# Routing the last sequence's softmax transposes through HBM in a one-core attention + mixture-of-experts kernel

## The chip, the cores and the metric

The kernel runs on 1 core of one Trainium2 chip. The metric is the device time of one execution in microseconds (us), as the median of several runs. Before the change it is 686.94 us, the median of 3 runs (684.95 to 687.5).

## The reference

All numbers are float32. Eight sequences of 512 tokens with 256 features go through causal attention, and then every token goes through one shared feed-forward expert and two of eight routed experts:

```python
x = x + attn(layernorm(x), Wq, Wk, Wv)        # x: (8, 512, 256); one head, scores / sqrt(256), causal softmax
h = layernorm(x)
shared = (silu(h @ shared_gate.T) * (h @ shared_up.T)) @ shared_down.T       # inner size 512
probs = sigmoid(h @ router_w.T + routing_bias)                                # 8 experts
scores, indices = top_k(probs, 2); scores = scores / sum(scores)              # weights w per token and expert
routed = sum over the two experts e of w_e * ((silu(h @ gate_w[e]) * (h @ up_w[e])) @ down_w[e])
out = x + shared + routed
```

## The kernel before

A sequence is four blocks of 128 tokens (`NT` = 4), and the 256 features are two chunks of 128 (`ND` = 2). Wq and Wk are folded into one matrix ahead of everything, so that a sequence needs one projection for its scores (`project_q`) and one for its values (`project_v`).

**First stage, one iteration per sequence b (0 to 7).** For each of its four blocks i, `attend` multiplies the transposed exponentials with the values ("average", tile `av`, with i + 1 pairs of matmuls), adds the result to the residual (`summed`, line 476), works out the second layer norm (statistics on VectorE, a power on GpSimd) and normalizes into `hn`. Scores and exponentials of sequence b + 1 are made at the end of iteration b. There are two ways to turn things around, because the array needs its contracted index on the partitions:

- on TensorE: `attend` transposes the exponentials block by block (line 463), and `turned` transposes `hn` (line 340); each result is copied out of PSUM by ScalarE;
- by HBM: the tile is written to HBM and read back in 32-row strips (`stored_rows`, `loaded_blocks`, `loaded_squares`), and VectorE then transposes 32 x 32 squares (`turn_squares`, `turn_exponentials`, line 434).

Three sets say which sequence goes which way. `SENT` are the sequences whose exponentials go by HBM: 1 to 6 before. `VIA` and `WHOLE` are those whose `hn` goes by HBM, its first half or all of it: `WHOLE` is 0 to 5; sequence 6 turns all of `hn` on TensorE, sequence 7 its second half.

**Routing.** The generator `chosen` runs `route` in pieces: logits on TensorE (`lT`, 16 records), their transpose (`pl`), the first of the two choices on VectorE, then the second choice and the running counts (`run`, line 535). `place` works out each token's row in a table in HBM (`pp`, `at`), and `dispatch` scatters the rows with eight indirect transfers from GpSimd (line 559, `rows_h`). Before, sequence 6 does its whole routing at once at the end of its iteration.

**The shared expert beside it.** `shared_beside` does the shared expert for half a sequence (a "unit"): for each of four chunks m a gate and an up product (`pg`, line 578; w = 0 and 1), a tanh on ScalarE (line 589) and two VectorE instructions ("gates", lines 593 and 596, the second writes `hid`), and then two down products (`po`, line 605), each copied by ScalarE (line 609, `marks["sh"]`). In the trace each 128-row float32 matmul is two records, so a unit is 32 records of `pg` and 16 of `po`. Sequences 0 to 3 and 7 have their units in the list `waiting`; sequences 4 to 6 store `hT` and get their shared expert after the routed experts. Before, one unit is done in each iteration 0 to 5 and one in iteration 7; the three that are left come after the loop, beside `plan_tiles`.

**After the loop.** `plan_tiles` counts tokens per expert, writes blank rows (line 199) and makes a table of tiles. Then come the routed experts, tile by tile: `fetch` loads a tile's rows from `rows_h` with four strip loads and a `tail` on SyncE's queue (lines 851, 856), and its two expert matrices of 512 KB with two loads on ScalarE's queue (line 838). The first tile's rows wait until all scattered rows have landed. `turn` transposes (line 873), `expert_up` multiplies (line 900), ScalarE takes the silu (line 885), VectorE the product (line 886), `expert_down` multiplies again (line 923). Rows and weights are fetched three tiles ahead; the weights of tiles 1 and on are issued behind the last unit's `marks["sh"]` on ScalarE:

```python
        with tc.issue_after(opening), tc.issue_after(marks["sh"]):
            items += [fetch(t)[1] for t in range(1, AHEAD)]
        with tc.issue_after(marks["hid"]):
            hT = turn(0, items[0][0])
```

**What sets the order.** The order on each engine is fixed when the program is built, by the order of the code and by a planner that takes ready work where an engine would be idle. `with tc.issue_after(ins)` puts the block's instructions behind `ins` on the engine of `ins`; instructions on other engines are not held. `marks` carries such points between functions. PSUM is shared by three pools: `ps_t` (2 buffers, transposes), `ps_m` (4, most products), `ps_o` (2; `av`, `lT`, `pl`, `pp`, `po`).

Of the kernel before, what the change touches and what calls it, by code (L numbers as in the profile page):

```python
# [26 lines left out]
def kernel(  # L27
# [45 lines left out]
    assert B == E, "each sequence's attention has one expert's down weights loaded beside it"  # L73
    EARLY = B // 2
    LATE = range(EARLY, B - 1)
    VIA = [b for b in range(B) if b != B - 2]
    WHOLE = range(B - 2)
    SENT = range(1, B - 1)

    BLOCKS = NT * (NT - 1) // 2, NT  # L80
    RS = 1.0 / D ** 0.5
# [194 lines left out]
    with ExitStack() as first, ExitStack() as inner:  # L276
# [181 lines left out]
        def attend(xb, i, ex, inv, v, mv, rstd, hn, meanwhile=None, exT=None):  # L458
            n = (i + 1) * P
            if exT is None:  # L460
                pt = ps_t.tile([P, S], F32, tag="t", name="pt")
                for j in range(i + 1):
                    nc.tensor.transpose(pt[:, ts(j, P)], ex[:, ts(j, P)], ident)
                exT = work.tile([P, S], F32, tag="exT", name="exT")
                marks["exT"] = nc.scalar.copy(exT[:, :n], pt[:, :n]).ins
            else:
                exT = part(exT, i)
            if meanwhile is not None:
                meanwhile()
            av = ps_o.tile([P, D], F32, tag="o", name="av")  # L470
            for j in range(i + 1):
                mixed = nc.tensor.matmul(  # L472
                    av, lhsT=exT[:, ts(j, P)], rhs=v[:, j, :], start=(j == 0), stop=(j == i)
                )
            with tc.issue_after(marks["turned"]) if "turned" in marks else nullcontext():
                summed = nc.vector.scalar_tensor_tensor(
                    out=xb[:, i, :], in0=av, scalar=inv, in1=xb[:, i, :], op0=ALU.mult, op1=ALU.add
                )
            stats_of(mv, xb[:, i, :], i)
            power = rstd_of(rstd[:, i : i + 1], mv[:, i : i + 1, :])  # L480
            if i:
                with tc.issue_after(summed.ins) if i != NT // 2 or xb is not total[B - 1] else nullcontext():
                    normalize(hn[:, i - 1, :D], xb, i - 1, mv, rstd)
            return mixed.ins, summed.ins, power

        def route(b, hT, hn):


            lT = ps_o.tile([P, P], F32, tag="o", name="lT")
            for k in range(ND):  # L490
                for c in range(NT):
                    marks["routed"] = nc.tensor.matmul(
                        lT[ts(c, P // NT), :], lhsT=r_sb[:, k, :], rhs=hT[:, k, ts(c, P)],
                        start=(k == 0), stop=(k == ND - 1),
                    ).ins
            logits = small.tile([P, P], F32, tag="logits", name="logits", bufs=2)
            nc.scalar.copy(logits, lT)
            yield
            pl = ps_o.tile([P, NT, P // NT], F32, tag="o", name="pl")
            marks["routed"] = nc.tensor.transpose(pl.rearrange("p c e -> p (c e)"), logits, ident).ins  # L500
            pl = pl[:, :, :E]
            wide = [P, NT, E]
            prob = small.tile(wide, F32, tag="prob", name="prob")
            nc.vector.tensor_tensor(out=prob, in0=pl, in1=bias_sb.unsqueeze(1).to_broadcast(wide), op=ALU.add)
            nc.scalar.activation(prob, prob, AF.Exp, scale=-1.0)
            nc.vector.tensor_scalar_add(prob, prob, 1.0)
            nc.vector.reciprocal(prob, prob)
            here = ts(b, NT)
            for r in range(TOP):
                top, hot = tops[r][:, here], hots[r][:, here, :]  # L510
                if r:
                    yield
                with tc.issue_after(marks["turned"]) if r and b < B - 2 else nullcontext():
                    nc.vector.tensor_reduce(out=top, in_=prob, axis=AX.X, op=ALU.max)
                nc.vector.tensor_tensor(
                    out=hot, in0=prob, in1=top.unsqueeze(2).to_broadcast(wide), op=ALU.is_equal
                )
                nc.vector.tensor_tensor(out=hot, in0=hot, in1=order, op=ALU.mult)
                win = small.tile([P, NT], F32, tag="win", name="win")
                nc.vector.tensor_reduce(out=win, in_=hot, axis=AX.X, op=ALU.max)  # L520
                nc.vector.tensor_tensor(
                    out=hot, in0=order, in1=win.unsqueeze(2).to_broadcast(wide), op=ALU.is_equal
                )
# [14 lines left out]
            yield mask  # L538
# [22 lines left out]
                    in_=hn[:, c, :], in_offset=None,  # L561
                ))

        def shared_beside(b, half, hT, midway=None, behind=None, rows_from=NI, early=None, steps=(), halfway=None):


            n = S // 2
# [5 lines left out]
            for m in range(NI):  # L573
                pg = ps_m.tile([P, 2, n], F32, tag="m", name="pg")
                for w in range(2):
# [6 lines left out]
                    if (m, w) in steps:  # L582
                        with tc.issue_after(mm.ins):
                            next(early, None)
                            held = marks["routed"]
                    elif (m, w) == (NI // 2 - 1, 1) and halfway is not None:
                        held = halfway
                sg = beside.tile([P, n], F32, tag="sg", name="sg")
                nc.scalar.activation(sg, pg[:, 0, :], AF.Tanh, scale=0.5)  # L589
                with nullcontext() if early is None or not 0 < rows_from < NI and m < rows_from else tc.issue_after(  # L590
                    marks["half"] if m >= rows_from else marks["coming"]
                ):
                    nc.vector.scalar_tensor_tensor(
                        out=sg, in0=sg, scalar=1.0, in1=pg[:, 0, :], op0=ALU.add, op1=ALU.mult
                    )
# [34 lines left out]
        for b in range(B):  # L630
# [27 lines left out]
            for i in range(NT):  # L658
# [2 lines left out]
                rest = None  # L661
                if b in SENT:
                    sc = exs[i]
                    if i % 2 == 0:
                        with tc.issue_after(mixed) if i else nullcontext():
                            qT = project_q(ahead_T, range(i // 2 * ND // 2, (i // 2 + 1) * ND // 2), qT if i else None)
                elif i + 1 < NT:
# [23 lines left out]
                if i == 1 and added is not None and b not in SENT:  # L691
                    with tc.issue_after(summed):
                        added()
                    added = None
                if i == (1 if b in SENT else 2) and placed is not None:
                    placed()


# [55 lines left out]
            def chosen(b=b, hT=hT, hn=hn):  # L754
# [5 lines left out]
                next(routing)  # L760
                yield
                next(routing)
                if b < B - 2:
                    yield
                mask = next(routing)

# [6 lines left out]
            if b + 1 < B:  # L773
                choice = chosen()
                next(choice)
                if b + 2 == B:
                    for _ in choice:
                        pass
            else:
                added = shared_beside(*waiting.pop(0), early=chosen(), rows_from=0, halfway=mixed, steps=((NI // 2, 1), (NI - 1, 0), (NI - 1, 1)))  # L780
            if b in LATE:
                with tc.issue_after(marks["sent"]):
                    nc.sync.dma_start(out=hT_d[b], in_=hT)
# [1 line left out]
                waiting += [(b, 0, hT), (b, 1, hT)]  # L785
            if b + 1 < B:

                if b + 2 < B:
                    def behind():

                        nonlocal exT
                        with tc.issue_after(marks["hid"]), tc.issue_after(marks["first"]):
                            exT = turn_exponentials(squares)
                        next(choice, None)
                        marks["squares"], marks["turned"] = marks["turned"], marks["run"]

                    def midway():
                        if b + 3 < B:
                            with tc.issue_after(marks["squares"]):
                                rows, _ = first_norm(*coming)  # L800
                            with tc.issue_after(marks["sent"]):
                                blocks[b + 3], _ = sent_to_blocks(xn_d[b + 3], rows)

                    added = shared_beside(
                        *waiting.pop(0), midway=midway, behind=behind, early=choice,
                        rows_from=1 if b in WHOLE else NI,
                        steps=((NI // 2, 1), (NI - 1, 1)) if b in WHOLE else ((0, 1), (1, 1)),
                    )
                xT = ahead_T
        placed()  # L810
        for c in to_send:
# [316 lines left out]
```

## Time and profile before

| what | value |
|---|---|
| median of 3 runs | 686.94 us |
| profiled execution, time | 678.78 us |
| profiled execution, span from first to last instruction | 677.0 us |
| granted TensorE clock over the span | 1.00 |
| busy share: TensorE, VectorE, ScalarE, GpSimd | 98%, 45%, 22%, 23% |
| first stage, iterations 0 to 6 | up to about 198 us |
| iteration 7, plan, last units | about 198 to 259 us |
| routed experts, late shared experts, sums | about 259 to 677 us |

A profile line gives times from the start of the span. In the chain of waits each line is start, duration, engine and line of the step that the end was waiting for. In the timeline each line is start, duration, engine and line, operation, output <- inputs, count and, in square brackets, how long the engine had been idle and what ended that. An engine with a "q" is its instruction queue issuing a transfer.

### The profile page before, as it was taken

What the parts mean: (1) busy time and instruction counts of PE and PEld (TensorE: products, weight loads), DVE (VectorE), ACT (ScalarE), POOL (GpSimd) and SP (SyncE); (2) the same over time, 40 slices, a digit from 0 to 9 for tenths busy, and PEclk for the clock granted to TensorE, in tenths of its full rate; (3) what the DMA queues carried; (4) which work ended last, traced back from release to release, by engine and by line L of the source; (5) the groups of instructions that cost most, each with busy time, mean ns of one, the idle gap of its engine ahead of it and who ended that gap; (6) DMA issues with size and microseconds to landing.
All of it is one profiled execution on the core that took longest, in us unless ns stands there. A gap on an engine that the chain in (4) does not pass through costs nothing.

```text
span 677.0 us, 10380 instructions
## 1 busy us (share of the span) xinstructions
PE 663.7 (98%) x3170; PEld 542.0 (80%) x3170; DVE 301.9 (45%) x1004; ACT 149.6 (22%) x357; POOL 157.2 (23%) x210
## 2 busy tenths in 40 slices
PE   7999999999999999999999999999999999999998
PEld 5677787777776888888888888888888899984556
DVE  4678879779786853212212212122122112223665
ACT  3433231332223222121111111211111111111110
POOL 3103351533526520022112121111211122120000
PEclk9999999999999999999999999999999999999999
DMA  7665777867834367776555354463543457714775
GB/s 237 192 166 147 219 210 178 220 180 209 218 115 134 106 163 226 230 199 209 162 167 170 119 180 150 138 180 127 161 161 102 159 172 239 259 65 146 244 226 177
DMA packets 155529, 119.52 MB, mean 177 GB/s; under 512 B 111856, under 2 KB 134000, under 8 KB 155472
## 3 DMA queue, kind: packets, MB, share of 16 engines
q1 hardware_dynamic: 136272, 58.05, 32.8%
q10 hardware_dynamic: 12912, 43.53, 18.5%
q0 software_dynamic: 6288, 17.24, 7.0%
q8 instruction: 28, 0.46, 0.3%
q14 instruction: 29, 0.24, 0.1%
HBM read 83.31 MB, written 35.47 MB: 175 GB/s over the span
## 4 chain that ended last, share of the span: by engine, by line
PE 78%; DVE 9%; DMA 6%; SPq 2%; issue 2%; POOL 1%; ACT 1%; ACTq 0%; DVEq 0%; POOLq 0%
PE po L923 17%; PE pg L900 16%; PE pu L900 16%; PE pg L578 7%; PE po L605 4%; PE pg L1011 3%; PE po L1070 3%; PE pu L1011 3%; PE av L472 3%; PE sc L442 2%; PE pm L407 2%; PE pm L395 2%; SPq L377 2%; DVE bnst L172 2%; DMA blocks<-hnd 2%
## 5 line engine op out<-in xcount | busy, mean ns | idle before, releaser
L886 DVE TENSOR_TENSOR hidp<-pu,sgt 128x512 f32<-128x512 f32 x56 | 38.5, 690 | 209.2 <-PE pu L900 194.4
L929 POOL DMA_INDIRECT rows_y<-y,to x56 | 53.6, 957 | 263.7 <-ACT y L928 155.2
L900 PE MATMUL pg<-hTt,w 128*128 128x256 f32 x448 | 105.8, 379 | 0.0
L900 PE MATMUL pu<-hTt,w 128*128 128x256 f32 x448 | 105.8, 379 | 0.0
L923 PE MATMUL po<-w_down,hidp 128*128 x448 | 101.4, 379 | 0.9 <-ACT y L928 0.9
L923 PEld LDWEIGHTS po<-w_down,hidp 128*128 128x128 f32 x448 | 85.0, 190 | 12.8 <-ACT y L928 1.4
L900 PEld LDWEIGHTS pg<-hTt,w 128*128 128x128 f32 x448 | 85.1, 190 | 11.6
L900 PEld LDWEIGHTS pu<-hTt,w 128*128 128x128 f32 x448 | 85.1, 190 | 11.6
L578 PE MATMUL pg<-hT,w_sh 128*128 128x256 f32 x320 | 73.8, 382 | 0.2 <-issue 0.2
L559 POOL DMA_INDIRECT rows_h<-hn,at x64 | 62.9, 983 | 22.7 <-issue 17.1
L885 ACT ACTIVATE sgt<-pg 128x512 f32<-128x512 f32 x67 | 39.8, 598 | 125.8 <-PE pg L900 122.2
L578 PEld LDWEIGHTS pg<-hT,w_sh 128*128 128x128 f32 x320 | 59.7, 190 | 9.5 <-ACT sg L589 1.0
L928 ACT COPY y<-po 128x256 f32<-128x256 f32 x67 | 24.9, 373 | 156.0 <-PE po L923 142.9
L179 POOL TENSOR_TENSOR rstd<-var,minus_half 128x1 f32<-128x1 f32 (+1 forms) x43 | 27.0, 636 | 125.7 <-DVE var L178 77.1
L605 PE MATMUL po<-w_sh,hid 128*128 128x256 f32 x160 | 37.5, 384 | 0.2
L442 PE MATMUL sc<-xT,qT 128*128 128x128 f32 (+3 forms) x128 | 37.4, 434 | 0.0
L605 PEld LDWEIGHTS po<-w_sh,hid 128*128 128x128 f32 x160 | 29.2, 190 | 6.8 <-DVE hid L596 2.5
L395 PE MATMUL pm<-xT,w_qk 128*128 128x512 f32 x64 | 30.1, 592 | 0.0
L886 DVE TENSOR_TENSOR khid<-pu,sgt 128x512 f32<-128x512 f32 x11 | 7.6, 691 | 49.2 <-PE pu L900 49.2
L407 PE MATMUL pm<-wv_sb,xT 128*128 128x256 f32 x128 | 29.0, 380 | 0.2 <-ACT xT L341 0.2
L407 PEld LDWEIGHTS pm<-wv_sb,xT 128*128 128x128 f32 x128 | 24.2, 190 | 6.1 <-issue 2.6
L172 DVE BATCH_NORM_STATS2 bnst<-total 128x6 f32<-128x256 f32 x64 | 25.1, 409 | 8.3 <-DMA total<-in_x_dram 8.3
(156 smaller groups left out, 755.7 us busy)
## 6 DMA issues: line engine op xcount, KB each, us to landing
w<-in_gate_w_dram ACTq DMA_DIRECT2D x41, 512.0 KB, 3.4
w<-in_up_w_dram ACTq DMA_DIRECT2D x41, 512.0 KB, 4.7
yl<-rows_y SPq DMA_DIRECT2D x32, 256.0 KB, 4.0
h<-rows_h SPq DMA_DIRECT2D x112, 64.0 KB, 3.3
w_down<-in_down_w_dram SPq DMA_DIRECT2D x8, 512.0 KB, 4.6
out_dram<-total SPq DMA_DIRECT2D x32, 128.0 KB, 2.7
total<-in_x_dram SPq DMA_DIRECT2D x7, 512.0 KB, 7.0
hnd<-hn SPq DMA_DIRECT2D x13, 256.0 KB, 2.2
```

What stands on the lines that cost most here:

```text
L395: nc.tensor.matmul(pm, lhsT=w_qk[:, k, ts(m, P)], rhs=xT[:, k, :], start=(k == 0), stop=(k == ND - 1),)
L407: nc.tensor.matmul(pm, lhsT=xT[:, k, ts(c, P)], rhs=wv_sb[:, k, :], start=(k == 0), stop=(k == ND - 1),)
L442: nc.tensor.matmul(sc[:, :n], lhsT=qT[:, k, ts(i, P)], rhs=xT[:, k, :n], start=(k == 0), stop=(k == ND - 1),)
L559: lands(nc.gpsimd.indirect_dma_start(out=rows_h[:, :], out_offset=bass.IndirectOffsetOnAxis(ap=at[:, r, c : c + 1], axis=0), in_=hn[:, c, ...
L578: mm = nc.tensor.matmul(pg[:, w, :], lhsT=w_sh[:, ds(w * gu + k * I + m * P, P)], rhs=hT[:, k, at], start=(k == 0), stop=(k == ND - 1),)
L605: nc.tensor.matmul(po, lhsT=hid[:, m, ts(j, P)], rhs=w_sh[:, ds(2 * gu + m * D, D)], start=(m == 0), stop=(m == NI - 1),)
L885: nc.scalar.activation(sg, pg, AF.Silu)
L886: return nc.vector.tensor_tensor(out=hid, in0=pu, in1=sg, op=ALU.mult).ins
L900: nc.tensor.matmul(dst[:, m, :], lhsT=w[:, i, k, ts(m0 + m, P)], rhs=hT[:, ts(k, n * P)], start=(k == 0), stop=(k == ND - 1),)
L923: nc.tensor.matmul(po, lhsT=hid[:, m, ts(j, P)], rhs=w_down[:, ds(w + m * D, D)], start=(m == 0), stop=(m == NI - 1),)
L929: nc.gpsimd.indirect_dma_start(out=rows_y[:, :], out_offset=bass.IndirectOffsetOnAxis(ap=to[:, j : j + 1], axis=0), in_=y, in_offset=None,)
L1011: nc.tensor.matmul(dst, lhsT=w_sh[:, ds(off + k * I + m * P, P)], rhs=hT[:, k, :], start=(k == 0), stop=(k == ND - 1),)
```

## The change

The three sets grow by one sequence: the exponentials of sequence 7 and all of `hn` of sequence 6 go by HBM. Iteration 6 then looks like the iterations before it: its routing is cut into pieces, and a unit of the shared expert runs in it, so two units are left after the loop where there were three. Sequence 7 turns all of its `hn` on TensorE. Its unit may start only its first chunk ahead of the last average (`halfway` after chunk 0, where it was after chunk 1), and its gates on VectorE stand behind the last average's sum (`gates_behind`).

```diff
     EARLY = B // 2
     LATE = range(EARLY, B - 1)
-    VIA = [b for b in range(B) if b != B - 2]
-    WHOLE = range(B - 2)
-    SENT = range(1, B - 1)
+    VIA = range(B - 1)
+    WHOLE = range(B - 1)
+    SENT = range(1, B)
...
             if i:
-                with tc.issue_after(summed.ins) if i != NT // 2 or xb is not total[B - 1] else nullcontext():
+                with tc.issue_after(summed.ins):
                     normalize(hn[:, i - 1, :D], xb, i - 1, mv, rstd)
...
-                with tc.issue_after(marks["turned"]) if r and b < B - 2 else nullcontext():
+                with tc.issue_after(marks["turned"]) if r and b < B - 1 else nullcontext():
                     nc.vector.tensor_reduce(out=top, in_=prob, axis=AX.X, op=ALU.max)
...
-        def shared_beside(b, half, hT, midway=None, behind=None, rows_from=NI, early=None, steps=(), halfway=None):
+        def shared_beside(b, half, hT, midway=None, behind=None, rows_from=NI, early=None, steps=(), halfway=None, gates_behind=None):
...
-                    elif (m, w) == (NI // 2 - 1, 1) and halfway is not None:
+                    elif (m, w) == (0, 1) and halfway is not None:
                         held = halfway
                 sg = beside.tile([P, n], F32, tag="sg", name="sg")
                 nc.scalar.activation(sg, pg[:, 0, :], AF.Tanh, scale=0.5)
-                with nullcontext() if early is None or not 0 < rows_from < NI and m < rows_from else tc.issue_after(
-                    marks["half"] if m >= rows_from else marks["coming"]
-                ):
+                first = marks["half"] if m >= rows_from else marks["coming"]
+                if early is None or not 0 < rows_from < NI and m < rows_from:
+                    first = gates_behind
+                with nullcontext() if first is None else tc.issue_after(first):
                     nc.vector.scalar_tensor_tensor(
...
                     sc = exs[i]
-                    if i % 2 == 0:
+                    if i % 2 == 0 and ahead_T is not None:
                         with tc.issue_after(mixed) if i else nullcontext():
                             qT = project_q(ahead_T, range(i // 2 * ND // 2, (i // 2 + 1) * ND // 2), qT if i else None)
...
-                if i == (1 if b in SENT else 2) and placed is not None:
+                if i == (1 if b in SENT and ahead_T is not None else 2) and placed is not None:
                     placed()
...
                 next(routing)
-                if b < B - 2:
+                if b < B - 1:
                     yield
                 mask = next(routing)
...
                 choice = chosen()
                 next(choice)
-                if b + 2 == B:
-                    for _ in choice:
-                        pass
             else:
-                added = shared_beside(*waiting.pop(0), early=chosen(), rows_from=0, halfway=mixed, steps=((NI // 2, 1), (NI - 1, 0), (NI - 1, 1)))
+                added = shared_beside(*waiting.pop(0), early=chosen(), rows_from=NI, halfway=mixed, gates_behind=summed, steps=((NI // 2, 1), (NI - 1, 0), (NI - 1, 1)))
...
             if b + 1 < B:
-                if b + 2 < B:
-                    def behind():
...
-                    def midway():
...
-                    added = shared_beside(
...
+                def behind():
...
+                def midway():
...
+                added = shared_beside(
...
```

The last hunk only takes `behind`, `midway` and the unit out of the inner `if`; their bodies are as before.

More of the change, by code (lines that the diff above doesn't have):

```diff
@@ L786 @@
             if b + 1 < B:
[L788 to L808 removed]
+                def behind():
+                    nonlocal exT
+                    with tc.issue_after(marks["hid"]), tc.issue_after(marks["first"]):
+                        exT = turn_exponentials(squares)
+                    next(choice, None)
+                    marks["squares"], marks["turned"] = marks["turned"], marks["run"]
+                def midway():
+                    if b + 3 < B:
+                        with tc.issue_after(marks["squares"]):
+                            rows, _ = first_norm(*coming)
+                        with tc.issue_after(marks["sent"]):
+                            blocks[b + 3], _ = sent_to_blocks(xn_d[b + 3], rows)
+                added = shared_beside(
+                    *waiting.pop(0), midway=midway, behind=behind, early=choice,
+                    rows_from=1 if b in WHOLE else NI,
+                    steps=((NI // 2, 1), (NI - 1, 1)) if b in WHOLE else ((0, 1), (1, 1)),
+                )
                 xT = ahead_T
```

## The prediction

> **What bounds the kernel now.** I read the page first: TensorE is busy 98% of the span.
>
> ```profile
> PE 663.7 (98%) x3170; PEld 542.0 (80%) x3170; DVE 301.9 (45%) x1004; ACT 149.6 (22%) x357; POOL 157.2 (23%) x210
> ```
>
> So TensorE's work or TensorE's few holes must change for the time to change. Next I read the windows, to find holes. From 300 to 580 us every 40 us window is 40.00 us busy: a shift ahead of 300 us passes on to the end whole, nothing later absorbs it. Iteration 7 is the loosest stretch (columns: window, length, then busy us and count for PE, PEld, DVE, ACT, POOL; clock, DMA share, GB/s):
>
> ```profile
> 198.20:217.60 19.40, 18.11 (x101) 13.80 (x100) 13.35 (x68) 6.13 (x17) 11.59 (x14) 1.00 0.28 100
> 217.60:227.60 10.00, 10.00 (x63) 8.45 (x62) 7.56 (x32) 2.46 (x7) 7.52 (x9) 1.00 0.35 112
> ```
>
> Then the chain of waits gives the calendar. Lines of iteration 5 (the model for iteration 6 after the change) and of the part that is rebuilt:
>
> ```profile
> 171.01 4.32 PE sc L442 x16
> ...
> 186.57 3.46 PE po L605 x16
> 190.03 1.72 PE pm L395 x4
> ...
> 198.22 0.45 PE sc L442 x4
> ...
> 215.78 1.86 PE av L472 x8
> 217.64 3.45 PE pg L578 x16
> ...
> 256.13 3.47 PE po L605 x16
> ```
>
> Last I read the timeline of SyncE's and ScalarE's queues where the routed experts begin, for what stands ready when the last unit ends:
>
> ```profile
> 247.05 1.96 SPq L851 DMA_DIRECT2D h<-rows_h  x4
> ...
> 250.11 1.86 SPq L851 DMA_DIRECT2D h<-rows_h  x4
> ...
> 253.46 1.85 SPq L851 DMA_DIRECT2D h<-rows_h  x4
> ...
> 256.48 7.31 SPq L851 DMA_DIRECT2D h<-rows_h  x4
> ```
>
> ```profile
> 263.45 0.37 ACTq L838 DMA_DIRECT2D w<-in_up_w_dram  x1
> 263.85 1.28 ACT L885 ACT_TABLE_LOAD   x1 [3.85 <-DMA w<-in_gate_w_dram]
> 265.15 0.60 ACT L885 ACTIVATE sgt<-pg 128x512 f32<-128x512 f32 x1
> ```
>
> Three tiles' rows are on chip before the first routed matmul (259.42), and the first silu waits behind six weight issues on ScalarE.
>
> **The change part by part.** The sum is made on the profiled execution: span 677.0 us and 1.78 us around it, 678.78. That lies 8.16 us (1.2%) under the median of 686.94; I carry the difference over to the median. About 0.5%, 3.4 us, is what a measurement of this kernel can tell from no change.
>
> *TensorE work.* Removed: ten transposes of exponentials and eight of sequence 6's `hn`; added: four more for sequence 7's. Fourteen fewer. Eight of them took 1.10 us at 201.96, 0.14 each: 1.9 us. A unit is 6.91 us (`pg`) plus 3.46 (`po`), 10.37, and only moves. The holes of iteration 7: the matmuls between 202.12 and 217.64 add up to about 13.3 us of 15.5, so 2.2 us of waiting for ScalarE and VectorE; these go too. If TensorE alone decided, the gain would be about 4 us at most.
> The Trainium skill, "TensorE: Matmul & The Clock Gate", Part 4, gives about 275 ns for a transpose in a kernel; fourteen would be 3.9 us, an estimate, and the cap 2 us higher. The trace's 0.14 decides.
>
> *End of the last average.* After the change iteration 6 runs like iteration 5: from `sc` (171.01) to the end of `po` (190.03) 19.02 us, so 198.22 + 19.02 = 217.24. The squares are turned on VectorE from 189.38 to 190.95 and the counts (`run`) end at 192.94; 27.21 us later these are 216.59, 218.16 and 220.15. In iteration 5 to 6 TensorE had 3.44 us of `project_q` to fill this; iteration 7 has none. Its averages 0 and 1 can start at 217.7, but each sum stands behind `run` on VectorE, and `ps_o` has two buffers: average 2 waits for the first sum (220.6), `pp` for the second, average 3 for the third sum. Average 2 takes 1.29 us (to 222.0), the third sum 0.48, average 3 1.72: 224.3, and 0.4 for VectorE's statistics in between (in iteration 6 the third sum came 0.6 us after its average). I take 224.7; 223.7 if `pp` comes after average 3, 225.3 if VectorE is later. Chunk 0 of the unit (1.72 us) fills the holes, as two groups of four records already do before (210.66, 214.75). It was 217.64: **7.06 us later**.
>
> *From there to the first routed matmul.* TensorE's own work after the last average was 41.96 us (217.64 to 259.60). Now it is one unit less, 0.5 us of transposes more: about 32, ending at 256.7, 2.7 us earlier than before. But the rows have their own chain: last sum, norm, `hn`, transposes, `lT`, `pl`, VectorE's two choices, places, eight scatters, landing, `h`. Before: first scatter 231.81, last one issued 241.15 and landed 246.54, first `h` issued 247.05, the fourth strip 248.69 and landed about 250.7 (1.9 later, the median in that window), VectorE's turn 0.7, about 251.7 for a first matmul: 34.05 after the last average, hidden then by 7.7 us of units. Now eight transposes and two copies lie in it in place of four and one: the start of eight to the end of `lT` was 2.35 us (201.96 to 204.31), to be set against four to `lT` before, +0.55. 224.7 + 34.6 = **259.3**, against 259.42. The cover of 7.7 us is gone, TensorE idles 2.6 us ahead of tile 0, and the gain of the moved unit with it: -0.1.
>
> *The prefetch.* The first `h` is issued at 254.66 in place of 247.05; the fourth tile's first strip landed 11.3 us after it (258.35), so at 265.96 at the earliest. In the trace the third tile's `up` weights (263.45) wait on the semaphore that this strip last used, and the silu of tile 0 is behind that issue. Issue 0.37, table load 1.28, silu 0.60: the first silu ends at 268.3. TensorE's tile 0 takes 6.9 us to 266.2, and tile 1's gate needs the PSUM buffer that this silu frees (4 in `ps_m`, all held by tile 0): **2.2 us** of hole. That is with 1.9 us per strip; with weights in flight strips took up to 7.8 us, which makes it 8.1. Bounds therefore 0 (if the semaphores fall otherwise, and ScalarE isn't held) to 8.1. Only one or two tiles' weights will be in flight here, not three, so I take about a third of the difference: 2.2 + 1.8 = 4.0.
> The Trainium skill, "DMA: Bandwidth & Descriptors", Anatomy of one DMA, gives about 2.0 us plus bytes by 436 GB/s (fitted for GpSimd's transfers): an estimate of 2.15 us for a 64 KB strip, loaded or not. The trace has 1.9 and 7.8 for the same strip. By the rule the hole is about 2.4 us and the whole sum +2.3, no measurable change; I go by the loaded row.
>
> *Edits at nothing.* Iteration 6's new transfers (two `hn` stores, eight strip loads, two stores of exponentials, eight square loads) take SyncE's queue for what iteration 5 shows from 170.8 to 186.7; behind them stand sequence 6's `hT` store and the last down weights, needed after 259 us. If the cover failed, `lT` would wait for `hn`'s second half, 0.5 us spare in iteration 5 (turned by 183.40, `lT` at 183.89). All eight scatters of sequence 6 now come after the last power on GpSimd: 10.2 us from about 227, done by 237.5, ahead of sequence 7's first at 239.4. The new `halfway` asks for what the planner does already: just chunk 0 ran ahead of the last average. The gates behind the last sum cost nothing, since all four chunks have a buffer; they may delay the norm by 0.4, and 0.7 is spare (`hn` ready 2.7 after the average, `pg` until 3.45). The one normalize that is now ordered behind its sum (0.41 us) has no reader before the transposes. VectorE loses four value copies (to ScalarE) and gains 1.57 us of squares.
>
> **Sum:** -0.1 + 4.0 = +3.9 us: 682.7 profiled, span 680.9, median **690.8**.
>
> **The rivals.**
> *A, nothing to measure.* The prefetch holds: semaphores fall differently or strips land in 2 us; -0.1 to +2.3, about 688. For it: TensorE's work is the same, and tile 0's start differs by 0.1. Against: ScalarE's queue is already 1 us from stopping TensorE there (first silu at 265.15, tile 1 at 266.33).
> *B, faster.* The row chain is 2.6 us shorter than I have it and hides behind the two units. Place: between the last average and the first `h`. It needs the last scatter to land after 4.0 us, as scatters in iteration 5 did, in place of 5.4 (-1.4), and the last average at 223.7 (-1.0). Then tile 0 starts at 256.7, -2.7, and with the 0.95 us hole at 283.76 (a copy behind a weight issue) gone, -3.7: 683.2. It decides when the first `h` is issued before 252.0. Against it: the first tile's weights and 1 MB of blank rows fly beside these scatters as before.
> *C, much slower.* Strips at 7.8 us: +8, 695.
> *D, it doesn't do what it says.* The planner fills iteration 7's holes with more than chunk 0; `halfway` forbids that, so I give it nothing.
>
> **How the numbers follow.** My case with C: 0.48, slower by over 0.5% (C about 0.12). A: 0.32, within 0.5%. B: 0.20, faster by over 0.5%. The range runs from B's 683.2 to 696, a little past C; the likeliest case alone 690.4 to 695.
>
> **What would show it.** Units after the loop: two; transposes of exponentials (line 463) 20 to 10, of `hn` (line 340) 12 to 8; averages from turned squares 120 to 140. Last average's end near 224.7, first `h` issue near 254.7, first routed matmul near 259.3 with 2.6 us idle before it, then a hole of some 4 us near 266 to 270 that a silu ends, behind a weight issue. I am wrong if the first `h` is issued before 252, or if tile 1 follows tile 0 without a hole.

## The result and the profile after

The changed kernel takes 688.2 us (median of 8 runs, 686.12 to 693.5); the kernel before, on the same chip, 685.17 us (8 runs, 683.61 to 687.5). The ratio on record, made from all these runs, is 1.0063, with an interval of 1.0038 to 1.0088: **4.3 us slower** (2.6 to 6.0); the two medians alone differ by 3.0 us. The forecast was 3.9 us slower.

The two profiled executions can't be subtracted from one another. The one of before took 678.78 us, under the lowest of its timed runs here; the one of after took 693.16 us, near the top of its own. So I also use a second profile of the same kernel before (687.02 us) and two more of the changed kernel (691.79 and 690.91 us). This table cuts each span at four events on TensorE: the first score product (`sc`) of sequence 7, the end of the last average, the first routed matmul, and the first down product of tile 10 (tiles counted from 0). All in us:

| profile | start to `sc` | to the last average | to the first routed matmul | to tile 10 | rest |
|---|---|---|---|---|---|
| before | 198.06 | 19.58 | 41.78 | 118.63 | 298.95 |
| before, second profile | 202.91 | 21.65 | 44.07 | 117.42 | 299.15 |
| after | 201.96 | 27.95 | 38.80 | 123.15 | 299.54 |
| after, second profile | 200.30 | 27.68 | 39.53 | 119.65 | 302.84 |
| after, third profile | 203.02 | 28.61 | 40.72 | 117.69 | 299.10 |

The last average ends later, as forecast. The stretch behind it, which has a whole unit (10.37 us) less in it, is shorter by only 3.4 to 5.3 us against the second profile of before. Part 1 of the page after the change shows that TensorE is busy longer, though it has fourteen instructions less (two stretches at half the clock, shown below, are part of that):

```profile
PE 668.5 (97%) x3156; PEld 542.4 (78%) x3156; DVE 305.1 (44%) x1003; ACT 147.7 (21%) x356; POOL 156.9 (23%) x210
```

The windows say where. For the changed kernel, from the first scores of sequence 7 to the last average, to `pp`, and to the first routed matmul (columns as in the prediction):

```profile
202.10:229.90 27.80, 26.24 (x131) 20.78 (x130) 19.03 (x76) 6.71 (x21) 10.51 (x13) 1.00 0.51 143
229.90:245.50 15.60, 12.04 (x72) 9.53 (x71) 9.20 (x39) 3.49 (x9) 8.33 (x9) 1.00 0.19 68
245.50:268.70 23.20, 22.01 (x96) 18.95 (x96) 14.19 (x63) 4.28 (x12) 7.78 (x8) 0.93 0.52 152
```

The second stretch has 3.6 us of idle TensorE, and the third has a granted clock of 0.93. The second profile of before, cut at its last average:

```profile
203.05:224.55 21.50, 18.22 (x101) 13.67 (x100) 13.34 (x68) 6.04 (x17) 11.61 (x14) 1.00 0.25 90
224.55:268.60 44.05, 42.92 (x212) 35.79 (x211) 27.34 (x110) 9.00 (x25) 15.25 (x16) 1.00 0.47 123
```

There the idle time stands ahead of the last average (3.3 us), and little behind it (1.1 us). TensorE's waits between 200 and 290 us name them (waiting line, releaser, sum, times, longest), first the changed kernel, then the second profile of before:

```profile
PE pg L897 <- ACT sgt L882: 3.7, 1, 3.7
PE pp L544 <- DVE mask L530: 3.5, 1, 3.5
PE av L472 <- DVE total L476: 1.6, 2, 1.0
PE pg L897 <- DVE hTt L870: 1.2, 1, 1.2
```

```profile
PE av L472 <- issue: 1.9, 1, 1.9
PE pl L500 <- ACT exT L465: 0.9, 1, 0.9
PE pp L544 <- DVE mask L530: 0.8, 1, 0.8
```

Of the four waits after the change I had forecast three: the averages behind VectorE's sums (1.6 us), tile 0 behind its rows (1.2), and tile 1 behind a silu (3.7). The 3.5 us ahead of `pp` I had not. The chain of waits of the changed kernel shows what lies in it (start, duration, engine and line):

```profile
229.91 3.45 PE pg L578 x16
233.37 0.94 PE pt L340 x8
...
235.18 0.57 PE lT L492 x16
...
238.11 5.24 another core or an unknown queue
...
243.43 0.38 ACT sh L610
...
244.16 0.39 ACT sh L610
...
244.58 0.69 DVE total L812
245.27 0.11 DVE mask L530
...
245.52 0.38 PE pp L544 x2
```

`pp` needs the mask of the routing; on VectorE the mask stands behind the sum of the unit's output (line 812), that sum behind ScalarE's copies of `po` (line 610), and those wait for TensorE's signal. The modelled records end the first `po` at 239.4 and the second at 240.7; the signals that release the copies came at 243.35 and 244.14, where no record ends, so the view calls the releaser unknown. The semaphore that the copies wait for is one that only TensorE's matmuls raise. The trace keeps the times at which it rose: for the six signals of these two `po` they are 238.37, 239.78, 241.19, 242.62, 243.35 and 244.14, where the modelled ends are 237.36, 237.79, 238.22, 238.65, 239.41 and 240.71. So TensorE's signals came up to 4 us after its modelled ends, and the lateness grew within `po` itself (the first four signals are 1.4 us apart, the modelled ends 0.43); whether the matmuls were late or only their signals, the trace doesn't tell.

And the forecast hole ahead of tile 1, in the timeline of the queues of SyncE and ScalarE in the changed kernel:

```profile
263.94 1.99 SPq L848 DMA_DIRECT2D h<-rows_h  x4
...
267.35 1.86 SPq L848 DMA_DIRECT2D h<-rows_h  x4
...
271.80 4.66 SPq L848 DMA_DIRECT2D h<-rows_h  x4
```

```profile
273.44 0.34 ACTq L835 DMA_DIRECT2D w<-in_gate_w_dram  x1
277.25 0.34 ACTq L835 DMA_DIRECT2D w<-in_up_w_dram  x1
277.62 1.28 ACT L882 ACT_TABLE_LOAD   x1 [9.67 <-DMA h<-rows_h]
278.25 0.34 ACTq L835 DMA_DIRECT2D w<-in_gate_w_dram  x1
278.91 1.09 ACT L882 ACTIVATE sgt<-pg 128x512 f32<-128x512 f32 x2
```

Two weight issues (273.44, 277.25) wait for strips of rows, and the table load and the silu stand behind them; a third (278.25), between the table load and the silu, waits for a strip too, and the chain goes through it. The strips took 3.90 and 6.43 us in the chain, not the 1.9 that the prediction took. When TensorE went on at 279.56, the first eight matmuls took 2.89 us and the next eight 2.52, in place of 1.73: a stretch of 3.413 us at half the clock (280.51 to 283.92) is on record there, and another (246.37 to 249.79) right behind the wait for `pp`. Each costs about 1.7 us, half its length (the two groups just named took 2.0 us more), and neither profile of before has one between the first 20 us and 600 us.

### The profile page after: what moved, and what is told of

Read it like the earlier page. It is cut to its first block, busy times and chain, and to the rows that moved or that the text cites. A ratio compares the mean times of both kernels' runs of the same rounds, so it can differ in the third digit from the quotient of the medians.

```text
span 691.4 us, 10366 instructions
## 1 busy us (share of the span) xinstructions
PE 668.5 (97%) x3156; PEld 542.4 (78%) x3156; DVE 305.1 (44%) x1003; ACT 147.7 (21%) x356; POOL 156.9 (23%) x210
## 4 chain that ended last, share of the span: by engine, by line
PE 84%; DVE 5%; DMA 3%; SPq 2%; issue 2%; another core or an unknown queue 1%; ACT 1%; POOL 1%; ACTq 0%; DVEq 0%
PE po L920 17%; PE pg L897 16%; PE pu L897 16%; PE pg L578 8%; PE sc L442 4%; PE av L472 3%; PE pm L407 3%; PE pg L1008 3%; PE po L1067 3%; PE pm L395 3%; PE pu L1008 3%; PE po L606 3%; DMA h<-rows_h 1%; PE lT L492 1%
## 5 line engine op out<-in xcount | busy, mean ns | idle before, releaser
L578 PE MATMUL pg<-hT,w_sh 128*128 128x256 f32 x320 | 76.0, 389 | 0.6 <-ACT v L411 0.5
L472 PE MATMUL av<-v,exTs 128*128 128x256 f32 x140 | 33.4, 384 | 1.6 <-DVE total L476 1.6
L472 PEld LDWEIGHTS av<-v,exTs 128*128 128x128 f32 x140 | 26.0, 190 | 7.8 <-issue 2.9
L589 ACT ACTIVATE sg<-pg 128x256 f32<-128x256 f32 x40 | 14.7, 384 | 69.7 <-PE pg L578 33.2
```

What stands on the lines that cost most here:

```text
L472: mixed = nc.tensor.matmul(av, lhsT=exT[:, ts(j, P)], rhs=v[:, j, :], start=(j == 0), stop=(j == i))
L578: mm = nc.tensor.matmul(pg[:, w, :], lhsT=w_sh[:, ds(w * gu + k * I + m * P, P)], rhs=hT[:, k, at], start=(k == 0), stop=(k == ND - 1),)
```

## The experiments

**First: where is it lost?** T1 puts the loss at the handover, where the routed experts take over from the units; T2 puts it into the rebuilt iterations 6 and 7. Four runs ask this: the kernel before without its last unit, the changed kernel with one unit done twice at the end, the changed kernel with a prefetch of two tiles in place of three, and the changed kernel once more.

```diff
 # before_unit_less (the kernel before)
-        while waiting:
+        while len(waiting) > 1:
 # after_unit_more (the changed kernel; its result isn't used)
+        shared_beside(*waiting[0])
 # after_ahead2 (the changed kernel)
-        AHEAD = 3
+        AHEAD = 2
```

> The kernel before without its last unit (the shared expert of the second half of sequence 7 is left out): two units after the loop, iterations 6 and 7 untouched. A unit is 10.37 us of TensorE. T1: only the 7.7 us of cover that the rows' chain does not need can be saved, and about 4 us come back as a hole behind the late prefetch, so the time falls by about 4 us (2.5 to 6). T2: nothing at the handover binds, so it falls by the whole 10.4 us.

> The changed kernel with one unit after the loop done twice (its second result is not added), so three units of cover again. T1: the added 10.37 us fill the holes at the handover (2.6 + 4 us by the prediction), so against the changed kernel the time rises by about 4 us only. T2: no holes to fill, it rises by 10.4 us.

> The changed kernel with rows and weights fetched two tiles ahead in place of three, so that the first silu stands on ScalarE behind four weight issues in place of six. T1: the first silu no longer waits for the fourth tile's strip; the hole ahead of tile 1 shrinks from 3.7 us to under 1, and the time falls by 2 to 4 us, to about that of the kernel before. T2: a shorter prefetch gains nothing; the same or slower by up to 2 us.

> The changed kernel once more, for a second profile. Theory T1 (the handover to the routed experts pays: rows and weights come later than the units cover): again a hole of 1 to 3 us ahead of tile 0, and again one of 2 to 5 us ahead of tile 1 that the first silu ends, behind a weight issue that waits for a strip of rows. Rival T2 (iterations 6 and 7 themselves got longer, and what the first profile shows at the handover was chance): tile 1 follows tile 0 without a hole, and the 3.5 us hole at the places of sequence 7 (line 544) comes again.

| kernel | median, us | ratio to before | interval |
|---|---|---|---|
| before_unit_less | 678.99 | 0.9918 | 0.9889 to 0.9946 |
| after_unit_more | 694.99 | 1.0139 | 1.0115 to 1.0162 |
| after_ahead2 | 688.77 | 1.0051 | 1.0029 to 1.0074 |

A unit is 10.37 us of TensorE. At the end it is worth only 5.6 us in the kernel before, and in the changed kernel one more costs 5.2 (1.0139 less 1.0063, of 685); the intervals make each of them uncertain by 2 to 3 us. Most of the rest hides the rows' way to the first tile. TensorE's timeline of the kernel with one unit less has the hole that the unit filled, and behind it a slow group, in which a half-clock stretch of 3.413 us is on record (about 1.7 us):

```profile
257.52 3.19 PE L900 MATMUL pg<-hTt,w 128*128 128x256 f32 x8 [2.33 <-DVE hTt L873]
```

The change takes a unit from the end, worth 5.6, and puts it into iteration 6. From the kernel with one unit less to the changed one it is 1.0063 less 0.9918, 9.9 us, against 10.37 for the unit. That is the price of the unit and of everything else in the change together, the fourteen transposes saved and the wait ahead of `pp` among it; the two kernels of the third set of runs (below) that have the unit in iteration 6 and no wait ahead of `pp` (1.0025 and 1.0024) give 7.3 us. Iterations 6 and 7 thus hid at most a part of the unit, and T2 holds for that side. With `AHEAD = 2` the wait ahead of tile 1 is gone, but the time is the changed kernel's (1.0051 against 1.0063, intervals overlapping): in that profile TensorE waits 2.0 us ahead of tile 0 and then runs at half the clock. The silu hole is also missing from the second and third profiles of the changed kernel (0.2 us and none). It comes and goes between executions.

**Second: VectorE's order.** T3 says that the wait ahead of `pp` is VectorE's order: the sum of line 812 stands ahead of the mask. So that sum is put behind the places; in another kernel the averages' sums are freed from the turned squares as well; in a third the unit of sequence 7 may again start two chunks ahead, and its gates are again written behind `marks["half"]`. That mark is not what it was: before the change it is the turning of sequence 7's own first half (line 384, at 220.77, behind the last sum); sequence 7 has left `VIA`, so now it is sequence 6's, long done, and the gates are freer than they were. The kernel before was profiled once more beside them.

```diff
 # after_sum_later, and after_sums_free
-        added()
+        with tc.issue_after(marks["placed"]):
+            added()
 # after_sums_free also
-            with tc.issue_after(marks["turned"]) if "turned" in marks else nullcontext():
+            with tc.issue_after(marks["turned"]) if "turned" in marks and xb is not total[B - 1] else nullcontext():
 # after_gates_free
-                    elif (m, w) == (0, 1) and halfway is not None:
+                    elif (m, w) == (NI // 2 - 1, 1) and halfway is not None:
...
-    early=chosen(), rows_from=NI, halfway=mixed, gates_behind=summed, steps=...
+    early=chosen(), rows_from=0, halfway=mixed, steps=...
```

> The kernel before once more, for a second profile: its first one (678.78 us) was some 6 us under its median. Expected near 684: the same order and waits, the difference in iterations 0 to 6 and at the end; no hole over 1 us between the last average and the first routed matmul, and no stretch of half clock there. If a hole of over 1 us stands there too, holes in that place are no mark of the change.

> The changed kernel with the sum of its last in-loop unit moved, on VectorE, from ahead of sequence 7's counts to behind its places. Theory T3 (the hole at line 544 is an order of VectorE: the counts stand behind a sum that waits for a late copy of the unit's down product): the hole of 3.5 to 4.1 us ahead of line 544 shrinks to under 1, the scatters start about 3.5 us earlier after the last average, the hole ahead of tile 0 closes, and the time falls by 3 to 5 us, to that of the kernel before or 1 to 2 us below. Rival T1 alone (only rows and weights at the handover count): the hole moves to another place, and the time falls by less than 1.5 us.

> The changed kernel with one part undone: the unit of sequence 7 may again start two chunks ahead of the last average, and its gates have no place given behind the last sum. If that part is worth nothing, as the prediction had it: within 1.5 us of the changed kernel. If the chain from the last average to the scatters decides (T1), four records more ahead of the last average and two pairs of gates ahead of the last norm make it 1 to 2 us slower.

> As after_sum_later, and the four sums of sequence 7 no longer stand behind the counts of sequence 6 on VectorE. The prediction has the last average end about 2 us later for that order. If so, the two waits for sums (0.54 and 1.02 us at line 472) go, the last average ends 1 to 2 us earlier, and with the chain the time falls by 1 to 2 us more than after_sum_later. If TensorE's work has become the limit again (no hole at the handover is left), it stays within 1 us of after_sum_later.

| kernel (another chip, before 687.19 us) | median, us | ratio to before | interval |
|---|---|---|---|
| after_sum_later | 697.14 | 1.0152 | 1.0123 to 1.0180 |
| after_gates_free | 694.99 | 1.0124 | 1.0091 to 1.0156 |
| after_sums_free | 696.84 | 1.0133 | 1.0096 to 1.0169 |

T3 falls. With the sum later the wait stays and has another name; TensorE's and ScalarE's timeline of that kernel:

```profile
246.12 0.41 PE L544 MATMUL pp<-mask,before 128*128 128x32 f32 x2 [3.38 <-ACT sh L610]
```

```profile
245.68 0.66 ACT L610 ACTIVATE sh<-po 128x256 f32<-128x256 f32 x2 [6.72 <-remote]
```

Now `pp` waits for a buffer of `ps_o`, which the same late copies hold. The order of the sum was not the cause; TensorE's lateness is ahead of both. This kernel is slower than the changed one by some 6 us, and its profile doesn't say why: TensorE's waits between 200 and 290 us add up to 8.6 us there, within those of the changed kernel's profiles. But the profile is the fastest of the seven runs (690.89 us, mean granted clock 0.998); the other six were granted 0.985 to 0.995. If time at half clock counts as half lost, an estimate, that is 1.4 us in the profiled run and 3.5 to 10 us in the others. Much of the 6 us is then the clock; which holes brought it, no trace shows.

With the unit's gates free, the wait ahead of the third average grows from 0.54 to 3.1 us (its TensorE timeline), because VectorE's and TensorE's room goes to the unit first:

```profile
230.55 1.56 PE L472 MATMUL av<-v,exTs 128*128 128x256 f32 x6 [3.10 <-DVE total L476]
```

VectorE's timeline there has two pairs of gates (224.88 and 226.61) ahead of the second turn of squares (227.40) and of `run`, which the averages' sums stand behind. So `halfway` after chunk 0 and `gates_behind`, undone together here, are needed: without them the rest of the change would cost about 4 us more (1.0124 against 1.0062 for the changed kernel on that chip), more than either theory expected. Freeing the averages' sums of the last sequence moved the wait forward instead: `pp` of sequence 6 then waits 4.8 us for its mask, and the time is that of after_sum_later.

**Third: why TensorE is late.** Two theories were left. T4: the eight transposes of `hn` and the sixteen thin logits products behind them. T5: the gaps ahead of the last averages. Three kernels, and the changed kernel beside them as the control.

```diff
 # after_half_via (the changed kernel)
-    VIA = range(B - 1)
+    VIA = range(B)
 # before_all_turned (the kernel before)
-    VIA = [b for b in range(B) if b != B - 2]
+    VIA = range(B - 2)
 # after_exps_turned: after_half_via, and also
-    SENT = range(1, B)
+    SENT = range(1, B - 1)
...
-                with tc.issue_after(marks["turned"]) if r and b < B - 1 else nullcontext():
+                with tc.issue_after(marks["turned"]) if r and b < B - 2 else nullcontext():
...
 # and the unit's gates and halfway as in after_gates_free
...
+                    if b + 1 in SENT:
                         with tc.issue_after(marks["hid"]), tc.issue_after(marks["first"]):
                             exT = turn_exponentials(squares)
```

> The changed kernel, but the first half of sequence 7's rows goes by HBM again, as it did before the change: four transposes of hn on TensorE ahead of sequence 7's logits in place of eight, everything else of the change kept. T4 (thin work): the block of eight transposes and sixteen thin logits products, run right after the gaps between the last averages, is what makes TensorE finish late in the down products of that unit (its signals came up to 4 us behind, a half-clock window was recorded at 246) and pp wait 3.5 us. Then the wait ahead of pp falls under 1.5 us, no half-clock window stands between 240 and 252, and the time falls by 2.5 to 4.5 us from the changed kernel's: ratio to before 1.000 to 1.003. T5 (gaps): the gaps ahead of the last averages themselves (0.5 and 1.0 us behind VectorE's sums) bring it, whatever is transposed. Then pp still waits 3 us or more and the ratio stays at 1.005 to 1.009.

> The changed kernel once more, as the control beside the other three on this chip. Both theories: ratio to before 1.004 to 1.009, a wait of 3 to 4 us ahead of pp, a half-clock window within 5 us of it.

> The kernel before, but all of sequence 7's rows are transposed on TensorE: eight transposes in place of four ahead of its logits, nothing else of the change (exponentials on TensorE, no unit in iteration 6). By work alone it costs 0.55 us of TensorE and saves two strip transfers' waits. T4: the eight transposes bring the late signals and the wait ahead of pp (3 us or more) and a half-clock window here too: ratio 1.004 to 1.007. T5: the gaps of the last averages are not there in this form, so pp waits under 1.5 us and the ratio is 0.999 to 1.002.

> Half of the change: sequence 6's hn by HBM, its routing in pieces and the unit in iteration 6 (so one fewer at the end), but sequence 7 as before the change: its exponentials are transposed on TensorE, the first half of its rows goes by HBM, two chunks of its unit may run ahead, its gates stand where they stood. By work: 8 transposes less than before (1.1 us), the unit moved (10.37 us each way), the end of the last average some 20 us after its first scores as before, 2.3 us of idle ahead of the first routed matmul as in the run with one unit less at the end. T4: neither eight transposes nor a wait ahead of pp over 1.5 us; ratio 0.999 to 1.004, within 0.002 of the run with half the rows by HBM. T5: the averages' gaps are gone, ratio 0.998 to 1.002, and lower by 0.003 or more than that run.

The last kernel leaves out the four loads of the second half of sequence 6's `hn`; sequence 5's stand in its place.

| kernel (before 686.88 us, 34 runs) | median, us | ratio to before | interval |
|---|---|---|---|
| after_third | 690.93 | 1.0062 | 1.0034 to 1.0089 |
| after_half_via | 688.34 | 1.0025 | 1.0000 to 1.0050 |
| after_exps_turned | 688.37 | 1.0024 | 1.0000 to 1.0049 |
| before_all_turned | 685.83 | 0.9988 | 0.9967 to 1.0009 |

With four transposes in place of eight the changed kernel is 2.5 us nearer to before (the two intervals overlap), and the wait ahead of `pp` is gone. VectorE's timeline of that kernel has the copies of `po` in time, and the mask ahead of the sum, so the planner's order there is another as well; ScalarE's timeline follows:

```profile
240.88 0.19 DVE L530 TENSOR_TENSOR mask<-hot,hot 128x32 f32<-128x32 f32 x1
241.38 0.69 DVE L812 TENSOR_TENSOR total<-total,sh 128x512 f32<-128x512 f32 x1 [0.31 <-issue]
```

```profile
238.80 0.38 ACT L610 ACTIVATE sh<-po 128x256 f32<-128x256 f32 x1 [1.66 <-PE po L606]
240.96 0.38 ACT L610 ACTIVATE sh<-po 128x256 f32<-128x256 f32 x1 [1.78 <-PE po L606]
```

The gaps ahead of the averages are the same there (1.6 us in all), so T5 alone falls. But T4 alone falls too: eight transposes in the kernel before cost nothing (0.9988), and `pp` waits 0.48 us in its profile. Late signals alone are no mark of the change either. In before_all_turned `pl` ends at 230.83 by the model, and VectorE, which had waited for it, reads it at 231.66:

```profile
231.66 0.19 DVE L504 TENSOR_TENSOR prob<-pl,bias_sb 128x32 f32<-128x32 f32 x1 [3.42 <-PE po L605]
```

By the record of the semaphore the signals between `lT` and the second `po` are up to 2.4 us late there, and up to 1.4 us in the second profile of before, but by the end of the second `po` they have caught up to within 0.7 us. Signals some 3 to 5 us late at the copies of `po`, and a wait of 3 us and more ahead of `pp`, were seen only with both: the changed end of iteration 7 and eight transposes in it. What makes TensorE late I can't say from these runs, nor whether the recording of the trace has a share in it. It stays open.

The profile of after_half_via still has a hole of 3.1 us that a silu ends, with a half-clock stretch at 275.6; its gain goes with the wait ahead of `pp` and the half-clock stretch behind that wait, neither of which it has. With the exponentials back on TensorE as well (after_exps_turned) the ratio is the same: sending the last exponentials by HBM adds or saves nothing that these runs can tell, though that kernel differs in its unit's order and in the loads it leaves out too. There TensorE had its largest wait in another place, behind sequence 6's logits, and a half-clock stretch at 218.97 behind it:

```profile
218.94 0.48 PE L500 MATMUL pl<-ident,logits 128*128 128x128 f32 x1 [2.48 <-ACT logits L497]
```

No version that does the whole work was faster than the kernel before by more than the interval.

## Why the prediction was right, and where it was not

The sign and the size were right (3.9 forecast, 4.3 measured), but the agreement in size is largely luck. The term that made the forecast, the prefetch, was 2.7 us too large in the mean of three profiles, and two terms that the sum did not have, the wait ahead of `pp` and the time at half clock, made up for it.

- **TensorE's work and the cap.** The work did fall: from `sc` to the first routed matmul TensorE's groups and holes give 60.5 us after (66.75 less 6.3 of holes, and 1.7 of it from a half-clock stretch) against 61.4 in the first profile of before, which has no hole there over 0.4 us. The holes of iteration 7 were not got rid of: 1.6 us stand ahead of the averages, and 3.1 to 3.8 more ahead of `pp`. They were also smaller than the 2.2 us of the prediction: the window that it shows has 1.29 us without a matmul (19.40 less 18.11).
- **The last average.** Forecast 26.6 us after `sc`, measured 27.7 to 28.6. The mechanism was as described: two holes, 0.54 and 1.02 us, each ended by a sum (line 476) that stands behind `run`. Against the second profile of before the delay is 6.0 to 7.0 us, and 7.06 was forecast.
- **From there to the first routed matmul: the step that failed.** Forecast 34.6 us with 2.6 us of idle ahead of tile 0; measured 38.8 to 40.7 with 0.9 to 1.9 of idle. The missing term is the wait ahead of `pp`, 3.1 to 3.8 us in every profile of the changed kernel: I took the row chain from before, where its `po` copies were in time, and added only the work of the four transposes (0.55 us). In after_half_via, where the wait is absent, the stretch is 36.4, and 35.9 in before_unit_less. The first `h` was issued at 263.94 in the first profile, not at 254.66; 3.9 us of that are the profile's own later `sc`.
- **The prefetch.** Forecast 4.0 us, bounds 0 to 8.1. Measured 3.7, 0.2 and none in three profiles of the same kernel, by the mechanism forecast (weight issue behind a strip's semaphore, then table load, then silu). So the term is a size that varies, about 1.3 in the mean, and not 4.0; the condition that I gave for being wrong, tile 1 following tile 0 without a hole, was met in two executions of three. The Trainium skill, "DMA: Bandwidth & Descriptors", Anatomy of one DMA, has a rule fitted for GpSimd's transfers, which would give an estimate of 2.15 us for such a strip; the chain shows 3.90 and 6.43 with weights in flight, and the measured rows decide.
- **Edits at nothing.** `halfway` and `gates_behind` I had at nothing, and no run shows that they cost anything. But the prediction missed what they are for: without them the averages wait 4.1 us in place of 1.6, and the time is about 4 us longer, since the mark that held the gates before no longer holds them.
- **Not in the sum at all: the clock.** Every profile of the changed kernel has two or more half-clock stretches of 3.413 us or one of twice that length behind its holes; each stretch of 3.413 us costs about 1.7 us. The runs without a kept trace have their mean granted clock on record, and it says the same. In the third set of runs it is 0.9934 in the mean of the changed kernel's twelve runs and 0.9983 in that of the 34 runs of before. With half the time at half clock counted as lost, an estimate, that is 4.5 us against 1.2 us: 3.4 of the 4.3 us by which the two mean times differ (up to 0.6 us of a run's share may stand at the very end of its span, as in the first profile of after). In after_half_via it is 0.9966, 2.3 us lost. By this estimate most of the loss reaches the time by way of the clock, as time lost behind the waits and not in them.

As a check on the new sum, from the profiles' waits between 200 and 290 us: 10.0, 7.5 and 6.4 us in the three of the changed kernel, 8.0 in the mean, against 4.3 in the second of before: +3.7. Two half-clock stretches, each an estimate of 1.7: +3.4. Fourteen transposes less: -1.9. Together +5.2, where the measurement has 2.6 to 6.0. Of the rivals, A's condition came about in two executions of three, when the prefetch held, and the time was lost at `pp` and by the clock instead. B needed the rows' chain to hide behind two units; before_unit_less shows that even in the order of before it doesn't: 2.3 us of idle ahead of tile 0.

## What to carry to other kernels

Before moving work away from a place where it stands ahead of a handover, price it by leaving it out: the unit of 10.37 us was worth 5.6 at the end, because most of the rest hid the rows' way to the first tile, and cost 7 to 10 with the rest of the change where it was put. A place that is "loose" because its steps wait for one another gives no room if the change makes them wait for something else there. And where a kernel keeps TensorE 98% busy, a hole of about 2 us and more should be priced with the half-clock stretch that may follow it.

## What the runs showed that I had not expected

- Holes on TensorE of about 2 us and more were often followed by a stretch of 3.413 us, or twice that, at half the granted clock. Of the holes from 3.1 to 4.8 us in all the traces only one had none (3.10 us, after_gates_free, ahead of the average). Of those from 1.9 to 2.5 us five had one: 2.33 us in before_unit_less (from 258.16), 2.02 in after_ahead2 (from 269.84), 1.92 and 2.28 in the second profile of after (from 268.2 and 619.77), 2.48 in after_exps_turned. Seven had none, among them 1.97 in after_half_via, 2.02 in after_exps_turned (at 618) and 2.35 in after_sums_free. The Trainium skill, "TensorE: Matmul & The Clock Gate", Part 1, states a free-running window of 3413 ns and at least one idle window before the clock drops; its length agrees with these records, but holes well under one window were enough here.
- TensorE's signals came up to 4 us after the modelled ends of its matmuls in the first profile of after, at the recorded full clock, and the profile then names the releaser as unknown or remote. The engines behind it did wait that long; the modelled ends alone do not show it.
- The same program differed by 8.2 us in span between two profiles (677.0 and 685.2) at a full recorded clock: 4.9 us of it ahead of sequence 7's first scores. The first of them, on which the prediction's sum was made, took 678.78 us, under every timed run of that kernel (683.4 and up), and it has no late signal between `lT` and the second `po`; the second has them.
